# The state's part of y in one float32r pass, two chunks at once, with D's product inside the addition

## The chip, the cores and the metric

The kernel runs on one core of one Trainium2 chip. The metric is the device time of one execution in microseconds (us), as the median of the runs. Five engines work side by side, each in its own order: TensorE (PE, with its weight loads listed as PEld), VectorE (DVE), ScalarE (ACT), GpSimd (POOL) and SyncE (SP), which here issues all DMA transfers. An engine takes its instructions in the order in which they were written and waits at an instruction until what that one needs is there.

## The reference

Input x is 8 sequences of 2048 tokens of 256 numbers. One layer is a Mamba-like mixer and a feed-forward part with weights and activations rounded to a 4-bit grid, each followed by a residual addition and a layer norm:

```python
xz = x @ W_in                                   # 256 -> 2 x 512
x_proj, z = jnp.split(xz, 2, axis=-1)
x_conv = silu(conv4(x_proj) + conv_b)           # 512 channels, four taps, causal
ssm = x_conv @ W_xproj                          # 512 -> 1 + 16 + 16
delta = softplus(ssm[..., 0])
Bm, Cm = ssm[..., 1:17], ssm[..., 17:]
h_mean = einsum('bld,bln->bdn', x_conv, delta[..., None] * Bm) / L
y = einsum('bdn,bln->bld', h_mean, Cm)          # the state's part of y
y = y + D * x_conv
x = layernorm(x + (y * silu(z)) @ W_out)
# gate, up and down: fp4_linear, 256 -> 704 -> 256, and the second layernorm
```

So h_mean, a matrix of 512 channels by 16 numbers for each sequence, is known only when all 2048 tokens of the sequence have gone through the convolution. Only then can the state's part of y be worked out for any of its tokens.

## The kernel before

**Tiles.** The tokens are taken in 32 blocks of 512, four to a sequence (a batch). Channels lie on the 128 partitions in four chunks (`NC` = 4). A block's steps up to the sums over tokens (`begin_block`) are done four blocks ahead (`LAG`) of its state and finish: `mix_block` adds the state's part, and `finish_pair` does two halves of 256 tokens (gating, output projection, layer norm, rounding to the 4-bit grid, gate, up, down, layer norm, store). Between the two, the convolved block waits in `xc`, and C in `ct`.

**Order.** Nothing is scheduled by rule: each step has a place in a table (`BLOCK` and `PAIR` for the steady part, `FIRST`, `BEGIN`, `END`, `FINAL`, `LAST`, `PREPARE` for the two ends). A place is a number on a scale on which one block is 64. All steps are sorted by it and written out in that order, which is the order of every engine's queue. The places are thus an order, not times.

**The steps around the change.**
- `x_projection` (line 860) leaves B, C and delta's input of a block in one PSUM bank of 128x128: 32 partitions for each of four groups of tokens, with C in the first 16. A token's group is given by bits 5 and 6 of its number, in pieces of 32 tokens.
- `keep_ssm` (line 870) copies that to `ct` with ScalarE.
- `sums` (line 954) adds delta*B times x_conv over a block's tokens in TensorE; dB, the product of delta and B, comes from VectorE (line 883).
- With the last block of a sequence, `mean` (line 964) and `low_mean` (line 968) split h_mean into a float32r part and a float32r remainder. `spread_mean` (line 981) adds the four groups and copies the sum to all four groups of 32 partitions, in two float32r matmuls of 512 columns. `keep_mean` (line 991) copies that to `hT`.
- `state` (line 1042) has, for each chunk and each group of tokens, one float32 matmul with 16 rows and 128 columns; the four groups use four row groups of TensorE and four PSUM banks. A float32 matmul shows as two records, a float32r matmul as one.
- `skip` (line 994) multiplies x_conv by D in place with ScalarE, a chunk at a time.
- `mix` (line 1053) adds a bank of the state's part to `xc` with VectorE, a group of tokens at a time.
- After that come `gated` (line 1107, GpSimd) and the output projection (line 1114).

Other lines that the text names: the taps of the convolution (834, VectorE), projections of x and z (814, 1091), gate and up (1140), down (1192), its tails in float32r (1202), `low_tails` (1180), a residual addition (774), the normalization ahead of the rounding (485), the 4-bit scales' way through DRAM to all partitions (`q_rows` at 548, then `xqT` or `hqT` at 555), the transposes of the rounded numbers (`q_gT`, 562) and GpSimd's product of the two (565).

Of the kernel before, what the change touches and what calls it, by code (L numbers as in the profile page):

```python
# [8 lines left out]
F32 = mybir.dt.float32  # L9
# [8 lines left out]
P = 128  # L18
# [15 lines left out]
    "load": -52.34,  # L34
    "halo": (-54.39, 2.45, -18.45, 6.59),
    "project": (-14.43, 9.80, 37.20, 16.89),
    "fetch": (-7.60, 24.33, 44.39, 30.03),
    "first": (11.35, 35.33, 60.30, 30.38),
    "tap": ((18.88, 21.74, 37.66), (52.75, 58.32, 69.30), (67.71, 70.25, 77.19), (50.68, 57.97, 63.17)),
    "silu": (53.41, 75.33, 79.81, 69.00),  # L40
    "skip": (190.70, 157.15, 101.00, 177.52),
    "x_projection": 84.55,
    "keep_ssm": 92.56,
    "by_token": 100.69,
    "negate": 97.98,
    "exp": 100.76,
    "ratio": 102.43,
    "series": (105.64, 108.25),
    "delta": 110.56,
    "delta_b": 114.03,  # L50
    "turn": (62.70, 87.06, 88.65, 77.94),
    "turned": (76.69, 88.95, 91.00, 81.01),
    "sums": 128.76,
    "mean": 129.42,
    "spread_mean": 131.69,
    "keep_mean": 133.74,
    "state": 70.98,
    "mix": (73.82, 73.78, 77.92, 79.02),
    "weigh": (96.23, 96.41, 93.68, 93.73),
    "split": (57.98, 77.03, 86.29, 75.12),  # L60
    "low_mean": 129.60,
}
PAIR = {
    "load_t": (16.12, 22.16),
    "load_x": (59.79, 95.09),
    "zed": ((39.34, 27.02), (56.07, 45.07)),
    "silu_z": ((47.44, 31.13), (65.03, 56.88)),
    "gated": ((85.61, 79.64), (91.67, 86.97)),
    "out": (90.71, 124.00),
    "residual1": (94.73, 128.83),  # L70
    "n1_rstd": (102.55, 136.22),
    "n1_apply": ((103.52, 106.41), (137.06, 137.46)),
    "q1_scales": (107.95, 145.44),
    "q1_normalize": (108.65, 146.84),
    "q1_magnify": (110.07, 147.67),
    "q1_add": (114.27, 150.04),
    "q1_subtract": (116.81, 151.46),
    "q1_turn_scales": (108.81, 147.79),
    "q1_spread_scales": (117.33, 152.86),
    "q1_turn": (118.33, 156.58),  # L80
    "q1_scale": (129.34, 158.98),
    "gate": ((142.14, 140.98, 133.76), (167.27, 176.12, 174.04)),
    "silu_g": ((147.06, 144.40, 151.72), (171.89, 183.70, 186.46)),
    "up": ((144.69, 150.12, 147.67), (176.40, 172.28, 186.36)),
    "product": ((150.32, 154.57, 154.57), (187.42, 185.28, 189.04)),
    "q2_scales": (154.89, 189.41),
    "q2_normalize": (159.20, 196.57),
    "q2_magnify": (165.48, 200.74),
    "q2_add": (168.70, 206.24),
    "q2_subtract": (169.55, 207.52),  # L90
    "q2_turn_scales": (155.72, 193.80),
    "q2_spread_scales": (168.31, 201.20),
    "q2_turn": (174.65, 214.51),
    "q2_scale": (186.08, 215.81),
    "down": ((194.72, 203.27), (219.29, 220.91)),
    "residual2": (210.68, 227.83),
    "n2_rstd": (215.57, 239.09),
    "n2_apply": ((218.44, 218.00), (239.70, 241.77)),
    "store": (221.27, 244.14),
    "q1_gather_scales": (111.97, 152.22),  # L100
    "q2_gather_scales": (162.03, 196.03),
    "tails": ((203.00, 205.74), (226.14, 222.82)),
    "n1_means": (95.59, 131.31),
    "n1_squares": ((101.45, 99.66), (135.48, 132.20)),
    "n2_means": (211.12, 229.92),
    "n2_squares": ((213.85, 212.29), (235.64, 236.97)),
    "high_tails": (192.49, 220.15),
    "low_tails": (194.36, 220.71),
}
FIRST = {  # L110
    "load": -68.17,
    "halo": (8.02, -7.73, -7.47, 25.64),
    "project": (17.61, -14.66, 43.74, 34.99),
    "fetch": (19.36, 4.81, 51.19, 41.72),
    "first": (25.39, 17.49, 51.37),
    "tap": ((35.57, 38.38, 40.53), (34.74, 35.93, 60.13), (59.04, 70.58, 74.19)),
    "silu": (66.52, 68.87, 80.32, 71.88),
    "skip": (121.16, 219.05, 107.21, 100.33),
    "x_projection": 91.94,
    "keep_ssm": 98.65,  # L120
    "by_token": 98.83,
    "negate": 98.77,
    "exp": 100.23,
    "ratio": 102.34,
    "series": (102.95, 104.55),
    "delta": 105.72,
    "delta_b": 112.06,
    "turn": (85.02, 88.88, 84.23, 87.79),
    "turned": (107.58, 93.45, 91.94, 98.83),
    "sums": 121.00,  # L130
    "mean": 121.27,
    "spread_mean": 125.37,
    "keep_mean": 126.33,
    "state": 66.04,
    "mix": (71.99, 70.80, 70.83, 73.53),
    "weigh": (95.37, 97.80, 93.25, 96.77),
    "convolve": (49.83,),
    "low_mean": 124.04,
}
BEGIN = {  # L140
    "load_t": (-77.09, -0.67),
    "load_x": (-76.08, -1.35),
    "zed": ((60.35, -73.21), (31.76, 70.11)),
    "silu_z": ((72.40, 11.73), (47.63, 78.40)),
    "gated": ((80.54, 80.69), (84.07, 88.27)),
    "out": (81.29, 92.27),
    "residual1": (86.38, 98.03),
    "n1_rstd": (94.57, 110.77),
    "n1_apply": ((97.02, 95.31), (116.96, 119.50)),
    "q1_scales": (98.07, 122.11),  # L150
    "q1_normalize": (100.88, 130.91),
    "q1_magnify": (105.57, 137.37),
    "q1_add": (108.48, 137.49),
    "q1_subtract": (109.59, 138.28),
    "q1_turn_scales": (99.62, 127.03),
    "q1_spread_scales": (123.41, 136.86),
    "q1_turn": (125.14, 143.90),
    "q1_scale": (130.91, 151.54),
    "gate": ((133.56, 135.76, 146.80), (165.06, 172.15, 159.36)),
    "silu_g": ((148.69, 138.88, 150.75), (166.63, 175.38, 168.87)),  # L160
    "up": ((146.37, 143.27, 150.92), (169.68, 167.71, 162.37)),
    "product": ((153.21, 144.84, 155.15), (176.04, 175.47, 174.33)),
    "q2_scales": (155.98, 176.26),
    "q2_normalize": (156.45, 183.04),
    "q2_magnify": (162.10, 190.53),
    "q2_add": (165.07, 205.06),
    "q2_subtract": (170.07, 208.78),
    "q2_turn_scales": (157.57, 180.44),
    "q2_spread_scales": (169.87, 205.54),
    "q2_turn": (171.21, 208.80),  # L170
    "q2_scale": (181.69, 214.91),
    "down": ((186.77, 192.27), (221.73, 218.85)),
    "residual2": (198.55, 224.24),
    "n2_rstd": (210.52, 248.03),
    "n2_apply": ((216.78, 217.63), (250.34, 248.54)),
    "store": (222.03, 255.31),
    "q1_gather_scales": (111.97, 130.96),
    "q2_gather_scales": (161.52, 194.72),
    "tails": ((196.33, 196.65), (222.82, 224.20)),
    "n1_means": (89.02, 102.14),  # L180
    "n1_squares": ((90.01, 89.31), (107.12, 107.30)),
    "n2_means": (200.27, 237.43),
    "n2_squares": ((202.63, 208.26), (239.28, 238.86)),
    "high_tails": (184.10, 219.50),
    "low_tails": (192.85, 220.11),
}
END = {
    "load_t": (39.80, 13.28),
    "load_x": (84.06, 104.01),
    "zed": ((41.20, 45.87), (75.26, 70.21)),  # L190
    "silu_z": ((44.31, 77.44), (86.40, 71.48)),
    "gated": ((71.40, 84.31), (99.83, 102.23)),
    "out": (90.92, 104.08),
    "residual1": (94.66, 118.60),
    "n1_rstd": (100.60, 122.75),
    "n1_apply": ((103.01, 106.23), (134.03, 135.73)),
    "q1_scales": (106.61, 139.28),
    "q1_normalize": (115.25, 147.28),
    "q1_magnify": (125.29, 148.05),
    "q1_add": (128.25, 151.13),  # L200
    "q1_subtract": (136.11, 152.97),
    "q1_turn_scales": (111.18, 139.87),
    "q1_spread_scales": (140.92, 155.72),
    "q1_turn": (142.30, 156.65),
    "q1_scale": (144.67, 159.64),
    "gate": ((148.01, 187.75, 209.32), (169.60, 163.63, 165.58)),
    "silu_g": ((150.66, 199.52, 212.85), (173.05, 197.11, 186.69)),
    "up": ((159.27, 174.74, 209.62), (171.44, 192.91, 187.62)),
    "product": ((176.55, 218.42, 251.49), (177.96, 200.34, 189.33)),
    "q2_scales": (254.96, 204.69),  # L210
    "q2_normalize": (255.50, 211.67),
    "q2_magnify": (294.36, 235.57),
    "q2_add": (295.01, 276.85),
    "q2_subtract": (318.60, 304.87),
    "q2_turn_scales": (256.75, 207.35),
    "q2_spread_scales": (316.27, 314.21),
    "q2_turn": (383.51, 327.55),
    "q2_scale": (415.11, 334.42),
    "down": ((507.19, 550.28), (361.85, 374.70)),
# [76 lines left out]
def mamba_fp4_ffn_kernel(  # L296
# [735 lines left out]
    def mix_block(n):  # L1032
# [24 lines left out]
        for t in range(TT):  # L1057
            at((n + LAG) * PERIOD, table, "mix", (t,), mix, t)
# [407 lines left out]
```

## Time and profile before

| | |
|---|---|
| median of 3 runs | 1766.36 us (1766.3 to 1766.78) |
| the profiled execution | 1770.15 us, its span 1768.4 us |
| granted TensorE clock | 0.997 |
| TensorE busy | 1736.7 us in 9646 records |
| VectorE busy | 1587.0 us |
| ScalarE busy | 1166.6 us |
| GpSimd busy | 778.3 us |
| state, line 1042 | 1024 records, 37.5 us busy |
| mix, line 1053 | 128 instructions, 83.7 us, 681 ns each |
| skip, line 994 | 128 instructions, 91.7 us, 717 ns each |

The span runs from the first to the last instruction of the profiled execution; the execution's own time has 1.75 us around it. Busy time of TensorE is the union of its records, whose ends are modelled: starts are the better measure there. Idle time of an engine is put down to whatever released it last.

### The profile page before, as it was taken

How to read it: one execution, taken by the hardware profiler on the slowest of the kernel's cores; microseconds unless marked ns; L12 is line 12 of the kernel's file. 1: busy time of each engine (PE TensorE's matmuls, PEld its weight loads, DVE VectorE, ACT ScalarE, POOL GpSimd, SP SyncE). 2: the span in 40 equal slices, each digit the busy share in tenths (PEclk: the TensorE clock that was granted, in tenths of full speed). 3: DMA queues.
4: the chain of work that ended last, by engine and by line, in shares of the span. 5: the costliest groups of instructions: out<-in, count | busy, mean ns of one | idle time of the engine just before them, and what ended most of it. 6: DMA issues, size and time to landing. Idle time of an engine off the chain costs nothing.

```text
span 1768.4 us, 28454 instructions
## 1 busy us (share of the span) xinstructions
PE 1736.7 (98%) x9646; PEld 1397.9 (79%) x9646; DVE 1587.0 (90%) x3081; ACT 1166.6 (66%) x2371; POOL 778.3 (44%) x840
## 2 busy tenths in 40 slices
PE   7999999999999999999999999999999999999997
PEld 3568787888877788788788888788888788888886
DVE  5998999998989999999999999999999999977786
ACT  5786767666767666767666767666777666654444
POOL 2333554444444444544444544444444444545443
PEclk9999999999999999999999999999999999999999
DMA  3244565555656555656655656554665545555443
GB/s 109 72 95 100 120 125 118 120 106 115 132 112 125 120 103 115 126 122 126 114 103 120 124 124 126 114 106 117 126 123 124 114 101 111 123 106 114 99 89 74
DMA packets 367473, 199.46 MB, mean 113 GB/s; under 512 B 290272, under 2 KB 342368, under 8 KB 367328
## 3 DMA queue, kind: packets, MB, share of 16 engines
q1 hardware_dynamic: 367328, 197.65, 53.5%
q8 instruction: 76, 1.25, 0.3%
q14 instruction: 69, 0.57, 0.1%
HBM read 116.34 MB, written 20.91 MB: 78 GB/s over the span
## 4 chain that ended last, share of the span: by engine, by line
PE 85%; DVE 8%; DMA 2%; ACT 2%; POOL 1%; issue 1%; SPq 0%; ACTq 0%; POOLq 0%; DVEq 0%
PE ps L1140 31%; PE ps L1192 14%; PE ps L1114 11%; PE ps L1091 11%; PE ps L814 10%; DVE xc L834 2%; PE ps L1042 2%; PE ps L1202 2%; PE hsum L954 2%; PE ps L860 1%; DMA hwT<-hw 1%; DVE xd L940 1%; DVE q_x L485 1%; DMA q_gT<-q_w 1%; DVE q_x L497 0%
## 5 line engine op out<-in xcount | busy, mean ns | idle before, releaser
L834 DVE SCALAR_TENSOR_TENSOR xc<-xp,cw_sb,xc 128x512 f32<-128x512 f32 x372 | 357.6, 983 | 9.7 <-ACT xc L828 9.1
L1140 PE MATMUL ps<-wuT,xqT 128*128 128x256 f32 (+1 forms) x1512 | 331.0, 363 | 1.5 <-ACT sg L1158 1.5
L1140 PE MATMUL ps<-wgT,xqT 128*128 128x256 f32 (+1 forms) x1512 | 326.5, 363 | 3.8 <-POOL xqT L565 3.8
L1140 PEld LDWEIGHTS ps<-wuT,xqT 128*128 128x128 f32 x1512 | 274.3, 190 | 46.2 <-issue 11.4
L1140 PEld LDWEIGHTS ps<-wgT,xqT 128*128 128x128 f32 x1512 | 273.5, 191 | 41.8 <-issue 12.2
L1192 PE MATMUL ps<-wdT,hqT 128*128 128x256 f32 x1260 | 290.7, 381 | 0.5 <-POOL hqT L565 0.5
L1192 PEld LDWEIGHTS ps<-wdT,hqT 128*128 128x128 f32 x1260 | 234.6, 190 | 51.8 <-issue 16.8
L1107 POOL TENSOR_TENSOR xc<-xc,sz 128x512 f32<-128x512 f32 x128 | 216.5, 1711 | 115.2 <-DVE xc L1053 115.2
L814 PE MATMUL ps<-xT,w_in_sb 128*128 128x512 f32 x512 | 245.9, 606 | 7.6 <-DMA xT<-in_x_t_dram 7.6
L1091 PE MATMUL ps<-xTz,w_in_sb 128*128 128x256 f32 x1024 | 242.1, 379 | 0.0
L1114 PE MATMUL ps<-w_out_sb,xc 128*128 128x256 f32 x1008 | 228.2, 379 | 2.2 <-DVE h L1165 1.9
L1091 PEld LDWEIGHTS ps<-xTz,w_in_sb 128*128 128x128 f32 x1024 | 194.0, 190 | 39.4 <-issue 14.4
L758 ACT ACTIVATE x<-x,ln_nb,ln_rs 128x256 f32<-128x256 f32 x256 | 142.4, 593 | 117.2 <-POOL ln_nb L755 97.6
L1114 PEld LDWEIGHTS ps<-w_out_sb,xc 128*128 128x128 f32 x1008 | 190.3, 190 | 28.7 <-issue 2.7
L565 POOL TENSOR_TENSOR hqT<-q_gT,hqT 128x1408 f32<-128x1408 bf16 x63 | 187.6, 2978 | 47.0 <-DMA q_gT<-q_w 40.0
L497 DVE SCALAR_TENSOR_TENSOR q_x<-q_w,q_x 128x512 f32<-128x512 bf16 (+3 forms) x131 | 156.1, 1192 | 39.8 <-ACT q_w L493 39.7
L493 ACT ACTIVATE q_w<-q_x 128x512 bf16<-128x512 f32 (+3 forms) x131 | 130.2, 994 | 86.8 <-DVE q_x L485 86.6
L907 ACT COPY xct<-hwT 128x1024 uint16<-128x1024 uint16 x112 | 130.0, 1161 | 83.1 <-DMA hwT<-hw 83.0
L814 PEld LDWEIGHTS ps<-xT,w_in_sb 128*128 128x128 f32 x512 | 94.0, 193 | 85.5 <-issue 77.7
L501 DVE SCALAR_TENSOR_TENSOR q_w<-q_w,q_x 128x512 bf16<-128x512 bf16 (+3 forms) x131 | 157.7, 1204 | 1.4
L565 POOL TENSOR_TENSOR xqT<-q_gT,xqT 128x512 f32<-128x512 bf16 x63 | 77.9, 1236 | 183.6 <-DMA q_gT<-q_w 173.5
L1165 DVE TENSOR_TENSOR h<-sg,ps 128x512 f32<-128x512 f32 (+1 forms) x189 | 116.7, 636 | 44.3 <-PE ps L1140 35.7
(137 smaller groups left out, 2548.9 us busy)
## 6 DMA issues: line engine op xcount, KB each, us to landing
hqT<-q_rows SPq DMA_DIRECT2D x63, 704.0 KB
xT<-in_x_t_dram SPq DMA_DIRECT2D x32, 512.0 KB
xTz<-in_x_t_dram SPq DMA_DIRECT2D x64, 256.0 KB
xt<-in_L_attn_x_dram SPq DMA_DIRECT2D x64, 256.0 KB
xqT<-q_rows SPq DMA_DIRECT2D x63, 256.0 KB
out_dram<-x SPq DMA_DIRECT2D x63, 256.0 KB
q_rows<-q_scT SPq DMA_DIRECT2D x252, 4.0 KB
q_rows<-q_scT SPq DMA_DIRECT2D x252, 12.0 KB
```

What stands on the lines that cost most here:

```text
L493: nc.scalar.activation(state["g"], state["x"], AF.Abs, scale=GRID)
L497: nc.vector.scalar_tensor_tensor(xn, w, 1.5 * GRID, xn, ALU.max, ALU.subtract)
L501: nc.vector.scalar_tensor_tensor(w, w, 1.5 * GRID, xn, ALU.max, ALU.subtract)
L565: nc.gpsimd.tensor_tensor(qT(), state["gT"], qT(), ALU.mult)
L758: nc.scalar.activation(r()[:, t, :], r()[:, t, :], AF.Identity, bias=v["nb"][:, t : t + 1], scale=v["rstd"][:, t : t + 1],)
L814: nc.tensor.matmul(mm, w_in_sb[:, k, c * P : (c + 1) * P], s["xT"][:, k, :], start=(k == 0), stop=(k == KM - 1),)
L834: nc.vector.scalar_tensor_tensor(acc, xp[:, k + 1 : k + 1 + T], cw_sb[:, c, k + 1 : k + 2], acc, ALU.mult, ALU.add)
L1091: nc.tensor.matmul(q["mm", j][:, a, :], w_in_sb[:, k, DI + c * P : DI + (c + 1) * P], q["xT"][:, k, :], start=(k == 0), stop=(k == KM - 1),)
L1107: nc.gpsimd.tensor_tensor(xc, xc, q["sz"][:, c, :], ALU.mult)
L1114: nc.tensor.matmul(mm[:, t, :], s["xc"][:, c, o : o + P], w_out_sb[:, c, :], start=(c == 0), stop=(c == NC - 1),)
L1140: nc.tensor.matmul(q[name, j][:, t, :n], q["xqT"][:, t * KM + k, :], wT[:, k, f0 : f0 + n], start=(k == 0), stop=(k == KM - 1),)
L1192: nc.tensor.matmul(q["d"][t], q["hqT"][:, t * (NF + 1) + j, :], wdT[t][:, t + j, :], start=(j == 0), stop=False,)
```

## The change

1. **C is split and spread.** `keep_ssm` still fills `ct`, for the transpose in `by_token` alone. `high` (ScalarE) copies the block's projection as float32r, `low` (VectorE) takes the remainder. `put_parts` writes C's two parts to DRAM in four transfers; some three blocks later `get_parts` reads them back in two transfers into `cs`: 64 partitions (16 numbers, by two parts, by two copies), 512 tokens in each row, and the same again in the other half of the partitions.
2. **h_mean is laid out to match.** `spread` now copies each of the 16 numbers to four rows in both halves of the partitions. `keep_mean` keeps the float32r part of all rows, and a new step `part_mean` (VectorE) turns the odd rows into the remainder. So the 64 rows of a half hold the four products of parts.
3. **state** is four float32r matmuls of 64 rows and 512 columns, one for each chunk, alternating between the lower and the upper half of the partitions. Each has a PSUM bank of its own.
4. **mix** goes by chunks, and multiplies `xc` by D as it adds: one `scalar_tensor_tensor`. `skip` is gone.
5. `xd` has two buffers instead of one, `ct` two instead of six, and **every table of places is new**.

```diff
 def keep_ssm():
-    s["ct"] = keep.tile([P, P], F32, tag="ct", name="ct")
-    nc.scalar.copy(s["ct"], s.pop("mm"))
+    s["ct"] = p2.tile([P, P], F32, tag="ct", name="ct")
+    nc.scalar.copy(s["ct"], s["mm"])
+
+def high():
+    s["hl"] = p2.tile([P, 2, P], F32, tag="hl", name="hl")
+    nc.scalar.copy(s["hl"][:, 0, :].bitcast(F32R), s["mm"])
+
+def low():
+    hl = s["hl"]
+    nc.vector.tensor_tensor(
+        hl[:, 1, :].bitcast(F32R), s.pop("mm"), hl[:, 0, :], ALU.subtract
+    )
+
+def put_parts():
+    s["parts"] = dram.tile([DS, 2, TT, P], F32, tag="parts", name="parts", bufs=LAG + 2)
+    hl = s.pop("hl")
+    for g in range(TT):
+        nc.sync.dma_start(s["parts"][:, :, g, :], hl[g * G : g * G + DS])
+
+def get_parts():
+    s["cs"] = p2.tile([P, TT, P], F32, tag="cs", name="cs")
+    rows = s.pop("parts").rearrange("n h g t -> (n h) (g t)")
+    for half in range(2):
+        nc.sync.dma_start(
+            s["cs"][half * 2 * G : (half + 1) * 2 * G].rearrange("p g t -> p (g t)"),
+            rows.unsqueeze(1).to_broadcast([G, 2, T]),
+        )
...
 def keep_mean():
-    hT_of[b] = p2.tile([P, DI], F32, tag="hT", name="hT", bufs=1)
-    nc.scalar.copy(hT_of[b], hs_of.pop("mm"))
-
-def skip(c):
-    nc.scalar.activation(
-        s["xc"][:, c, :], s["xc"][:, c, :], AF.Copy, scale=dk_sb[:, c : c + 1]
-    )
+    hs_of["high"] = p2.tile([P, 2, DI], F32, tag="hs", name="h_high", bufs=1)[:, 0, :]
+    nc.scalar.copy(hs_of["high"].bitcast(F32R), hs_of["mm"])
+
+def part_mean():
+    hT_of[b] = p2.tile([P, DI], F32, tag="hT", name="hT", bufs=1)
+    nc.vector.scalar_tensor_tensor(
+        hT_of[b].bitcast(F32R), hs_of.pop("high"), low_rows, hs_of.pop("mm"),
+        ALU.mult, ALU.add,
+    )
...
 def state():
-    s["y"] = [bank().rearrange("p (c n) -> p c n", n=P) for _ in range(TT)]
-    for c in range(NC):
-        for t in range(TT):
-            g = slice(t * G, t * G + DS)
+    s["y"] = [bank() for _ in range(NC)]
+    cs = s.pop("cs").rearrange("p g (t r) -> p t g r", r=G)
+    for j in range(NC // 2):
+        for half in range(2):
+            c = half * (NC // 2) + j
+            g = slice(half * 2 * G, (half + 1) * 2 * G)
             nc.tensor.matmul(
-                s["y"][t][:, c, :],
-                hT_of[b][g, c * P : (c + 1) * P],
-                s["ct"][g, :],
+                s["y"][c],
+                hT_of[b][g, c * P : (c + 1) * P].bitcast(F32R),
+                cs[g].bitcast(F32R),
                 start=True, stop=True,
             )

-def mix(g):
-    xc = s["xc"].rearrange("p c (t g r) -> p g c t r", g=TT, r=G)[:, g]
-    y = s["y"][g].rearrange("p c (t r) -> p c t r", r=G)
-    nc.vector.tensor_tensor(xc, xc, y, ALU.add)
+def mix(c):
+    xc = s["xc"][:, c, :]
+    nc.vector.scalar_tensor_tensor(
+        xc, xc, dk_sb[:, c : c + 1], s["y"][c], ALU.mult, ALU.add
+    )
```

The new `spread` and `low_rows` (minus one in odd rows, zero in even ones) are made once at the start by three small VectorE instructions more.

## The prediction, made before the changed kernel ran

> **What bounds the kernel now.** I read the page first (busy shares, the 40 slices, the chain that ended last), then the waits of TensorE, then stretches of the span, then TensorE's order of work around the lines that change.
>
> ```profile
> span 1768.4 us, 28454 instructions
> PE 1736.7 (98%) x9646; PEld 1397.9 (79%) x9646; DVE 1587.0 (90%) x3081; ACT 1166.6 (66%) x2371; POOL 778.3 (44%) x840
> PE 85%; DVE 8%; DMA 2%; ACT 2%; POOL 1%; issue 1%; SPq 0%; ACTq 0%; POOLq 0%; DVEq 0%
> ```
> TensorE is busy 98% of the span, and the chain runs through it for 85%. What an instruction on another engine costs matters only if TensorE then waits.
>
> The busy time of each engine in a stretch of the middle, in the order TensorE, weight load, VectorE, ScalarE, GpSimd, with clock, DMA share and GB/s:
> ```profile
> 200.00:460.00 260.00, 260.00 (x1460) 210.26 (x1459) 240.47 (x466) 180.01 (x363) 119.62 (x124) 1.00 0.59 118
> ```
> There TensorE never stops, at full clock, and a block takes 53.0 us. VectorE works 92.5% of that, 49.0 us a block: 4 us of room. TensorE's idle 31.7 us lie at the two ends of the span; the waits name 7.6 for the first load and 4.0 for dB at the start, and 1 to 2 each at the end.
>
> The price of the state's part is in TensorE's timeline (start, us, line, what, count):
> ```profile
> 545.68 1.46 PE L1140 MATMUL ps<-wgT,xqT 128*128 128x192 f32 x8
> 547.08 1.17 PE L1042 MATMUL ps<-ct,hT 16*128 16x128 f32 x32
> 548.18 1.98 PE L814 MATMUL ps<-xT,w_in_sb 128*128 128x512 f32 x4
> ...
> 515.96 4.48 PE L1192 MATMUL ps<-wdT,hqT 128*128 128x256 f32 x20
> 520.09 0.83 PE L1202 MATMUL ps<-wd_parts,parts 128*128 128x256 f32 x4
> 520.76 1.88 PE L814 MATMUL ps<-xT,w_in_sb 128*128 128x512 f32 x4
> ```
> A float32 matmul is two records. From start to start the 32 records of line 1042 take 1.10 us. The eight of 192 columns ahead take 1.40, though elsewhere in the steady part eight of them take 1.30, and a run of ten of line 1192 after such a state takes 2.26 (1675.03 to 1677.29) where 2.15 is usual. So the state costs TensorE 1.10 + 0.10 + 0.11 = 1.31 us a block. Its work proper, eight rounds of four row groups at once, each round 256 column steps, is eight times 0.115 = 0.92 us by the price of such steps below; the other 0.4 us go to entering and leaving.
>
> **The change, part by part.**
>
> *State in float32r, two halves of rows at once.* A float32r matmul is one record. Line 1202 is the nearest row: 20 records of line 1192 at 0.2155 last until 520.27, so the four float32r passes of 256 columns fill 520.27 to 520.76, 0.12 each; 512 columns are 0.23 to 0.24 (line 981, the only 512-column float32r row, gives 0.46 for two by the same reckoning). The four new passes use rows 0 to 63 and 64 to 127 alternately. Two at once: two rounds, 0.46 + 0.40 = 0.86 us. Bounds: 0.46 without any entering and leaving; 4 x 0.23 + 0.40 = 1.32 if the halves don't run together. I take 0.86, since line 1042 itself shows row groups together (32 records of over 0.1 us of steps in 1.10 us). Saved: 1.31 - 0.86 = 0.45 us a block, times 32 blocks: **-14.4 us**, at most -27.
>
> A rule of the Trainium skill speaks against a part of it. The row: while line 1202 runs, its weight loads (0.19 us each) start 0.12 to 0.19 us apart with passes of the same rows in flight, so a load is hidden.
> "TensorE: Matmul & The Clock Gate", Part 3, says that a weight load overlaps matmuls in flight only where the row group differs. By it the third pass would wait for its 0.19 us load, and 6 us of the 14.4 would be lost.
> I go by the row.
>
> *D joins the addition.* ScalarE loses 128 activations of 0.717 (line 994), 91.7 us; it gains 32 copies of 128x128 (row of line 870: 0.258), 8.3 us. It has a third of its time free, so nothing on the path. VectorE's four additions a block become multiply-adds of the same size: line 1053 takes 0.681, line 968 (the same form, 512 wide, one operand in PSUM) 0.690: +1.2 us in all. The nearest row that could be dearer is line 834, 0.983 with both operands in SBUF, which would be +39; but lines 968 and 774 read PSUM as the new one does and never exceed 0.70 and 0.43.
>
> *Split of C.* VectorE gains 32 subtractions of 128x128: between 0.28 (line 1180, 64x128) and 0.69 (line 968, 512 wide); I take 0.29, 9 us in all. Ahead of the transposes and additions in its queue that is 0.3 us in 4 of room: no cost. Without that room it would be 9 us.
>
> *The way through DRAM.* Six more transfers a block on SP: four writes, as line 548's four (1.7 to 2.6 us of issue), and two reads of 128 KB each. The writes stand behind the store and ahead of the q_rows and xt issues, and wait for the subtraction; the reads stand between the q_rows issue and the issue of xqT, which waits for q_rows anyway:
> ```profile
> 637.23 1.73 SPq L548 DMA_DIRECT2D q_rows<-q_scT  x4
> 639.85 0.40 SPq L1217 DMA_DIRECT2D out_dram<-x  x1
> 640.43 0.62 SPq L555 DMA_DIRECT2D xqT<-q_rows  x1
> 643.09 1.23 SPq L562 DMA_TRANSPOSE q_gT<-q_w  x1
> ```
> xqT is issued 2.6 us before the transpose that GpSimd's product also needs, and that product ends 3 to 6.7 us before TensorE uses it. One microsecond later costs nothing; without cover it would be 1 us a block, 32 us. The q_rows behind the writes feed hqT, whose issue (625.90) came 8 us before its transpose's (634.47). The reads come some three blocks after their writes.
>
> *The start of a batch.* The state of its first block waits for hT, and the way there gets one step longer, a VectorE multiply-add of 0.69 (row of line 968), behind the copy. Before:
> ```profile
> 1547.65 0.81 PE L981 MATMUL ps<-hs,spread 128*128 128x512 f32 x2
> 1548.30 1.46 PE L1140 MATMUL ps<-wgT,xqT 128*128 128x192 f32 x8
> 1549.70 1.17 PE L1042 MATMUL ps<-ct,hT 16*128 16x128 f32 x32
> ...
> 1548.50 0.59 ACT L991 COPY hT<-ps 128x512 f32<-128x512 f32 x1 [0.47 <-PE ps L981]
> 1548.61 1.63 DVE L485 TENSOR_TENSOR q_x<-h,q_rs 128x1408 f32<-128x1408 f32 x1
> ```
> hT was there at 1549.09. In the new order VectorE runs low_mean, then that 1.63 us normalization, then the new step. Low_mean ended at 1547.76, so the new step runs from 1549.4 to 1550.1. TensorE, with two more passes of line 1202 ahead of the state (0.24 us), is ready at 1549.8: a wait of 0.3 us, eight times: **+2.4 us**. Bounds 0 and 1.6 (another such operation) each: 0 to 13.
>
> *New places.* The steady order keeps its distances. Adding TensorE's rows: from the end of the output projection to the first gate matmul 30.5 and 33.4 us by halves (30.5 and 32.2 before), from the last up matmul to the first down 33.0 and 33.8 (31.8 and 29.1 before), from the state to the output projection 15.4 (15.5). At the start, block 0's x projection stands 10.8 us ahead of its sums instead of 8.6, which should give back some 2 of the 3.7 us that TensorE waits there. At the end the last pairs have 1 to 2 us less between up and down; I count +2. Together 0, with 4 either way.
>
> **Sum.** -14.4 + 2.4 = -12.0. The profiled execution took 1770.15 (span 1768.4 and 1.75 around it), so 1758 for one like it; it lies 3.8 above the median of the runs, 1766.36. That median less 12.0 is 1754.4: **1754.5 us**.
>
> **The rivals.**
> 1. *The halves don't run together, or the 128-byte pieces in which a pass reads C halve its pace.* Line 860 reads such pieces without loss, but in float32, at half the rate of columns. The state then costs 1.32, nothing is won, and the start of a batch adds 2.4: 1769. For it: no row here shows 64-row groups. Against: line 1042 shows four row groups together.
> 2. *The batch starts eat the gain.* VectorE arrives a whole long operation late at each: 8 x 1.6 = 13 us, so 1766. Against: only the queue's next operation stands there, of known length.
> 3. *VectorE becomes the bound* (slower). It goes from 49.0 to about 49.5 us a block. Its twelve taps a block average 0.98 us, between 0.65 and 3.4, whatever their equal shape; the long ones lie beside other engines' work. If new neighbours raise that mean, the blocks follow VectorE once it needs 52.6, a mean of 1.24; beyond 1.32 the kernel is slower than before. At 1.35 it needs 53.9, 0.9 over the old period in 28 steady blocks: 1791. For it: 4 us of room and every place new. Against: TensorE's waits on VectorE in the steady part are zero now, and ScalarE and GpSimd get no more work.
>
> **How the numbers follow.** A measurement of this kernel tells differences over about 0.2% (3.5 us) from none. Forecast 0.68, its own range 1746 to 1763 (the run at 0.6 to 1.0, ends 4 either way); rival 1 0.12, rival 2 0.05, rival 3 0.15. Faster: the forecast and 0.03 of rivals 1 and 2 in part, 0.71. Same: 0.12. Slower: rival 3 and the worst of rival 1, 0.17. The range reaches to rivals 1 and 2, 1745 to 1772, and leaves rival 3 out.
>
> **What would show it.** Right: the state as four records that start in two close pairs, with about 0.66 us from its start to the next line's in place of 1.10, TensorE's share still 98%, steady period 52.5 us, small waits on hT at batch starts. Wrong: four records 0.23 apart (rival 1), waits on hT of over 1 us (2), a tap mean over 1.2 us and TensorE waiting for VectorE in the middle (3), or TensorE waiting for the read-back C or for xqT, which would put the six transfers on the path.

## The result, and the profile after

The changed kernel takes 1788.0 us (median of 4, 1785.8 to 1789.2) beside 1766.6 us for the kernel before: a ratio of 1.0119, with a 95% interval of 1.0102 to 1.0137. It is slower by 21 us, where 12 us less were forecast. The profiled execution took 1786.9 us, its span is 1785.1 us, the granted clock 0.994.

The head of the page and the shares of the chain that ended last, after:

```profile
span 1785.1 us, 26935 instructions
PE 1732.8 (97%) x8750; PEld 1383.5 (78%) x8750; DVE 1658.4 (93%) x3123; ACT 1099.8 (62%) x2275; POOL 794.5 (45%) x840
DVE 49%; PE 22%; ACT 12%; issue 9%; POOL 4%; DMA 3%; SPq 0%; DVEq 0%; ACTq 0%; POOLq 0%
```
TensorE's part of the chain fell from 85% to 22%, VectorE's rose from 8% to 49%. VectorE is busy for 71 us more than before, though the new instructions are few and small.

The same stretch of the middle as in the prediction, and TensorE's timeline around a state (line 1098 now):

```profile
200.00:460.00 260.00, 253.71 (x1289) 201.79 (x1288) 250.85 (x455) 165.25 (x335) 117.36 (x118) 1.00 0.62 124
```
```profile
544.97 0.53 PE L1259 MATMUL ps<-wd_parts,parts 128*128 128x256 f32 x2
545.44 0.73 PE L1098 MATMUL ps<-cs,hT 64*128 64x512 f32 x4
546.10 1.99 PE L1197 MATMUL ps<-wgT,xqT 128*128 128x256 f32 x8
```
The state is what the forecast said: four records that start in two close pairs, 0.34 us apart, and 0.66 us from its start to the next line's (545.44 to 546.10) in place of 1.10. But TensorE, which never stopped in this stretch before, now stops for 6.3 us of it, and VectorE works 96.5% of it.

Where VectorE's 71 us went is in its groups with shapes kept apart (busy us, mean ns). The lines of before, then of after; each second line is the subtraction of the first quantization, line 501 before and 520 after:

```profile
L834 DVE SCALAR_TENSOR_TENSOR xc<-xp,cw_sb,xc 128x512 f32<-128x512 f32 x372 | 357.6, 983 | 9.7 <-ACT xc L828 9.1
L501 DVE SCALAR_TENSOR_TENSOR q_w<-q_w,q_x 128x512 bf16<-128x512 bf16 x63 | 49.2, 781 | 0.2
L1053 DVE TENSOR_TENSOR xc<-xc,ps 128x512 f32<-128x512 f32 x128 | 83.7, 681 | 7.8 <-PE ps L1042 7.4
```
```profile
L853 DVE SCALAR_TENSOR_TENSOR xc<-xp,cw_sb,xc 128x512 f32<-128x512 f32 x372 | 334.7, 920 | 8.5 <-ACT xc L847 8.2
L520 DVE SCALAR_TENSOR_TENSOR q_w<-q_w,q_x 128x512 bf16<-128x512 bf16 x63 | 134.5, 2134 | 1.2
L1108 DVE SCALAR_TENSOR_TENSOR xc<-xc,dk_sb,ps 128x512 f32<-128x512 f32 x128 | 91.9, 741 | 14.4 <-PE ps L1098 14.3
L897 DVE TENSOR_TENSOR hl<-ps,hl 128x128 fp32r<-128x128 f32 x32 | 8.3, 258 | 0.2
```
The new work (line 897, 8.3 us; 8.2 us more in the additions; 5.9 us for the part of the mean) is some 22 us. The taps got shorter. One instruction that the change does not touch, the subtraction of line 520, went from 0.78 to 2.13 us and took 85 us more: 33 of its 63 now last over 2.5 us, where 2 did before.

Its neighbours show why. GpSimd's and VectorE's timelines of after, at the same time (start, us):

```profile
614.50 2.87 POOL L584 TENSOR_TENSOR hqT<-q_gT,hqT 128x1408 f32<-128x1408 bf16 x1
```
```profile
614.52 3.40 DVE L520 SCALAR_TENSOR_TENSOR q_w<-q_w,q_x 128x512 bf16<-128x512 bf16 x1
617.85 1.14 DVE L1222 TENSOR_TENSOR h<-sg,ps 128x512 f32<-128x512 f32 x2
```
The subtraction lasts until 0.55 us after GpSimd's product into `hqT` is over. Alone it takes 0.68 us. So it stood still for about 2.7 us, and the profile counts that as busy time. The next pair of products waits behind it. In the kernel before, the subtraction (line 501) was out of the way when that product (line 565) began:

```profile
615.53 0.70 DVE L501 SCALAR_TENSOR_TENSOR q_w<-q_w,q_x 128x512 bf16<-128x512 bf16 x1
617.78 1.15 DVE L1165 TENSOR_TENSOR h<-sg,ps 128x512 f32<-128x512 f32 x2 [1.55 <-PE ps L1140]
```
```profile
617.03 2.88 POOL L565 TENSOR_TENSOR hqT<-q_gT,hqT 128x1408 f32<-128x1408 bf16 x1
```
There GpSimd's product lay in a gap of VectorE and beside two products with one operand in PSUM, which took no longer than elsewhere. Other `hqT` products held a tap, then as now at the cost of some 2.7 us (23 taps of over 2.5 us before, 15 after): those are the longest taps of the prediction.

### The profile page after: what moved, and what is told of

It reads as the page before. It is cut to its first block, busy times and chain, and to the rows that moved or that the text cites. A ratio compares the mean times of both kernels' runs of the same rounds, so it can differ in the third digit from the quotient of the medians.

```text
span 1785.1 us, 26935 instructions
## 1 busy us (share of the span) xinstructions
PE 1732.8 (97%) x8750; PEld 1383.5 (78%) x8750; DVE 1658.4 (93%) x3123; ACT 1099.8 (62%) x2275; POOL 794.5 (45%) x840
## 4 chain that ended last, share of the span: by engine, by line
DVE 49%; PE 22%; ACT 12%; issue 9%; POOL 4%; DMA 3%; SPq 0%; DVEq 0%; ACTq 0%; POOLq 0%
DVE xc L853 11%; PE ps L1197 8%; DVE q_x L516 5%; DVE q_am L483 5%; DVE q_w L520 4%; DVE h L1222 4%; DVE xd L984 4%; DVE q_x L504 3%; PE ps L1249 3%; ACT xct L951 3%; PE ps L833 3%; PE ps L1148 3%; PE ps L1171 2%; DVE q_sc L490 2%; DVE x L793 2%
## 5 line engine op out<-in xcount | busy, mean ns | idle before, releaser
L1197 PE MATMUL ps<-wgT,xqT 128*128 128x256 f32 (+1 forms) x1512 | 337.9, 367 | 5.3 <-issue 3.5
L853 DVE SCALAR_TENSOR_TENSOR xc<-xp,cw_sb,xc 128x512 f32<-128x512 f32 x372 | 334.7, 920 | 8.5 <-ACT xc L847 8.2
L1197 PE MATMUL ps<-wuT,xqT 128*128 128x256 f32 (+1 forms) x1512 | 324.3, 361 | 0.0
L1164 POOL TENSOR_TENSOR xc<-xc,sz 128x512 f32<-128x512 f32 x128 | 223.2, 1755 | 119.6 <-DVE xc L1108 119.5
L584 POOL TENSOR_TENSOR hqT<-q_gT,hqT 128x1408 f32<-128x1408 bf16 x63 | 192.9, 3061 | 119.6 <-DMA q_gT<-q_w 82.2
L520 DVE SCALAR_TENSOR_TENSOR q_w<-q_w,q_x 128x512 bf16<-128x512 bf16 (+3 forms) x131 | 242.2, 1849 | 1.4
L770 POOL TENSOR_SCALAR ln_ve<-ln_var 128x2 f32<-128x2 f32 (+1 forms) x130 | 50.9, 392 | 288.4 <-ACT ln_sq L759 282.8
L1159 ACT ACTIVATE sz<-ps 128x512 f32<-128x512 f32 x128 | 76.0, 593 | 143.9 <-PE ps L1148 143.4
```

The source lines that it names most:

```text
L520: nc.vector.scalar_tensor_tensor(w, w, 1.5 * GRID, xn, ALU.max, ALU.subtract)
L584: nc.gpsimd.tensor_tensor(qT(), state["gT"], qT(), ALU.mult)
L853: nc.vector.scalar_tensor_tensor(acc, xp[:, k + 1 : k + 1 + T], cw_sb[:, c, k + 1 : k + 2], acc, ALU.mult, ALU.add)
L1164: nc.gpsimd.tensor_tensor(xc, xc, q["sz"][:, c, :], ALU.mult)
L1197: nc.tensor.matmul(q[name, j][:, t, :n], q["xqT"][:, t * KM + k, :], wT[:, k, f0 : f0 + n], start=(k == 0), stop=(k == KM - 1),)
```

## The experiments

Theory P: the new places put a VectorE instruction beside GpSimd's product that holds it; the change's own arithmetic is as cheap as forecast. Rival W: the change gives VectorE more work than it has room for. All kernels of this section were timed against the kernel before (medians 1766.4 to 1767.4 us). "Start", "middle" and "end" split the span at the first matmul of the fifth and of the last block's state, as the trace has them. "Batch start" and "other" are the mean intervals from one state to the next over 22 blocks, beginning at the fifth: the 5 intervals that lead to the first block of a new sequence, and the other 17. VectorE's busy time and the subtraction's mean are in us.

| kernel | us | ratio (95%) | VectorE busy | subtraction, mean | start | middle | end | batch start | other |
|---|---|---|---|---|---|---|---|---|---|
| before | 1766.4 | | 1587 | 0.78 | 281.2 | 1392.7 | 94.5 | 53.43 | 53.10 |
| after | 1788.0 | 1.0119 (1.0102 to 1.0137) | 1658 | 2.13 | 275.1 | 1415.7 | 94.3 | 57.09 | 53.18 |
| e1, places alone | 1790.9 | 1.0133 (1.0118 to 1.0148) | 1643 | 1.90 | 277.8 | 1412.6 | 95.6 | 55.60 | 53.40 |
| e2, arithmetic alone | 1781.2 | 1.0086 (1.0069 to 1.0103) | 1575 | 0.70 | 286.2 | 1399.0 | 94.7 | 55.31 | 52.93 |
| e3, products first | 1753.9 | 0.9927 (0.9912 to 0.9942) | 1617 | 1.41 | 271.0 | 1388.2 | 95.6 | 54.22 | 52.60 |
| e4, no hqT product | 1740.8 | 0.9852 (0.9836 to 0.9869) | 1543 | 1.20 | 267.1 | 1378.9 | 92.8 | 53.05 | 52.58 |
| e5, hqT on VectorE | 1772.1 | 1.0026 (1.0015 to 1.0037) | 1607 | 0.70 | 271.8 | 1394.3 | 104.1 | 55.19 | 52.66 |
| e6, mean earlier | 1748.7 | 0.9898 (0.9881 to 0.9914) | 1617 | 1.47 | 268.6 | 1381.2 | 94.4 | 53.40 | 52.61 |
| e7, e5 and e6 | 1761.4 | 0.9969 (0.9959 to 0.9980) | 1605 | 0.70 | 272.7 | 1385.2 | 104.2 | 53.74 | 52.60 |
| e8, mean earlier alone | 1778.2 | 1.0065 (1.0050 to 1.0080) | 1663 | 2.19 | 270.4 | 1411.4 | 94.6 | 54.93 | 53.62 |
| e9, gating first | 1754.7 | 0.9931 (0.9914 to 0.9948) | 1619 | 1.45 | 273.9 | 1386.7 | 93.2 | 54.25 | 52.58 |
| e10, mixed orders | 1748.0 | 0.9890 (0.9874 to 0.9906) | 1607 | 1.25 | 271.5 | 1381.9 | 92.8 | 53.40 | 52.58 |
| e11, part of the mean first | 1769.9 | 1.0021 (1.0010 to 1.0033) | 1571 | 0.70 | 284.8 | 1388.5 | 93.3 | 53.53 | 52.85 |

**e1: the new places, without the new arithmetic.** The kernel of before, with every table of the changed kernel (`skip` keeps its own places). In its first block the gating of the first half comes ahead of the last of the four additions, since the new tables go by chunks.

> The kernel of before, with the changed kernel's places for every step that both have; no new arithmetic. Theory P (the new places: the VectorE subtraction of q1 stands beside GpSimd's product into hqT and lasts until that is over): the subtraction's mean goes from 0.78 us to 1.5 to 2.2 us, VectorE's busy time from 1587 us to 1630 to 1660 us; TensorE still needs its old 53.2 us a block, so that most of this lies beside it, and the time is 1768 to 1782 us. Theory W (the change's own VectorE work - the remainder of C, D inside the mix, the part of the mean - is too much for VectorE): the subtraction stays at 0.78 us, VectorE at 1587 us within 10, the time at 1766 us within 4.

Measured 1790.9 us. The subtraction's mean is 1.90 us and VectorE is busy for 1643 us, as P said and W did not. The time is above P's range: I had counted the holds as lying beside TensorE's 53.1 us. TensorE waits at the batch starts instead, 55.6 us there beside 53.4 us. There is no added link in this kernel, yet TensorE stops for 8.1 us in all, in `spread_mean`, until VectorE has the remainder of the mean. So the places alone, on old arithmetic, cost 24 us.

**e2: the new arithmetic, with the old places.**

```diff
 BLOCK (all other places as before)
+    "high": 93.24, "low": 95.07, "put_parts": 97.46, "get_parts": 311.72, "part_mean": 134.20,
+    "mix": (73.78, 77.92, 73.82, 79.02),
-    "skip": ...
```

> The changed kernel's arithmetic, with the places of before for every step that both have, and the new steps (the two parts of C, their store and read-back, the part of the mean) put in where the changed kernel has them relative to their neighbours. P: the subtraction's mean is 0.7 to 0.9 us, VectorE is busy for 1590 to 1615 us, TensorE's state passes are 0.44 us shorter a block, and the time is 1750 to 1762 us, 5 to 16 us under before. W: VectorE is busy for 1640 us or more and the time is 1780 us or more, as in the changed kernel.

Measured 1781.2 us, where W put it (1780 us or more) and above P's range. But W's reason is not there: VectorE is busy for 1575 us, less than before, and the subtraction takes 0.70 us. The blocks within a sequence take 52.93 us, 0.17 less than before. The loss is elsewhere: 5 us in the first blocks, and at the batch starts, where TensorE waits for the new link of the mean's chain. TensorE's timeline, then VectorE's:

```profile
928.95 0.80 PE L1098 MATMUL ps<-cs,hT 64*128 64x512 f32 x4 [1.74 <-DVE hT L1039]
```
```profile
925.96 1.62 DVE L504 TENSOR_TENSOR q_x<-h,q_rs 128x1408 f32<-128x1408 f32 x1
927.50 0.74 DVE L853 SCALAR_TENSOR_TENSOR xc<-xp,cw_sb,xc 128x512 f32<-128x512 f32 x1
928.16 0.74 DVE L1039 SCALAR_TENSOR_TENSOR hT<-h_high,low_rows,ps 128x512 fp32r<-128x512 f32 x1
```
This is the second rival of the prediction, under the old order: the part of the mean stands behind a normalization and a tap, and the state's matmuls wait 1.7 us. Three of these waits are followed by 3.4 us in which the granted clock is 0.50, which takes another 1.7 us each.

**e11: the same, with the normalization behind the part of the mean.** `"q2_normalize"` of the second half goes from 196.57 to 198.21.

> The changed kernel's arithmetic with the places of before (1781.2 us), and on VectorE the normalization of the second half's second quantization (1.62 us) moved behind the new part of the mean, which it stood ahead of. There the state's matmuls waited 1.7 to 2.2 us for hT at seven batch starts, and the block before a start took 54.8 to 57.2 us. If the new link of the chain, queued behind that normalization, is what costs there: 53.0 to 53.6 us at the starts and 1767 to 1774 us in all. If the rest (the first blocks, single blocks of 54.3 us) weighs more, or the wait only moves to another matmul: 1777 to 1782 us.

Measured 1769.9 us, 11 us less than e2. The batch starts fall from 55.31 to 53.53 us. One place of one instruction, which runs once a block, decided whether the added link was on the path. It is still 3.5 us over the kernel before: the start is 3.6 us longer and a block takes 52.85 us, not 52.58. What keeps it there was not taken apart.

**e3: VectorE's order around the subtraction.** In the second half of a block the subtraction goes behind the two products; in the first half behind the products and ahead of two taps.

```diff
-    "q1_subtract": (117.96, 153.46),
+    "q1_subtract": (122.06, 158.28),
-    "q1_turn": (126.15, 155.03),
+    "q1_turn": (126.15, 158.29),
-    "tap": (..., (49.63, 54.48, 64.97), ..., (51.31, 54.87, 64.83)),
+    "tap": (..., (49.63, 58.10, 64.97), ..., (51.31, 58.20, 64.83)),
```

> The changed kernel, with only VectorE's order around the two q1 subtractions of a steady block altered: the two products of gate and up, which read one operand from PSUM, go ahead of the subtraction, so that they and not the subtraction run beside GpSimd's product into hqT (in one of the two places two taps also move behind the subtraction). No work is taken away. P: the subtraction still waits for the rest of hqT's product, but about 1.1 us of it is used twice a block; the subtraction's mean falls from 2.13 to 1.2 to 1.7 us, VectorE is busy for 1590 to 1625 us, and the time is 1758 to 1774 us. W: the work is the same, so the time stays at 1788 us within 4 and VectorE at 1658 us within 10.

Measured 1753.9 us, below P's range, 34 us under the changed kernel, with the same instructions. VectorE's busy time fell by 42 us, and W falls.

**e9: GpSimd's order alone.** The changed kernel with one place moved: in one half of a block the gating (1.3 us) goes ahead of `hqT`'s product. The orders of the other engines are untouched.

```diff
-    "q2_scale": (185.89, 217.49),
+    "q2_scale": (185.89, 222.20),
```

> The changed kernel (1788 us) with one place altered, on GpSimd's queue alone: in one of the two halves of a block the gating product (1.3 us) goes ahead of hqT's product (2.9 us). VectorE's, ScalarE's and TensorE's orders are those of the changed kernel. H (a VectorE instruction with both operands in SBUF is held for as long as GpSimd's product runs): in that half the q1 subtraction stands beside the gating instead and is held for 1 us and not 2.7 us; hqT's product then runs beside the two products with a PSUM operand and the maximum, which are not held; the subtraction's mean falls from 2.13 us to 1.2 to 1.7 us and the time to 1766 to 1780 us. O (the products-first kernel was faster only because VectorE reads the gate and up results out of PSUM earlier): VectorE's order is unchanged here, so the subtraction and the time stay, 1788 us within 3.

Measured 1754.7 us: 33 us under the changed kernel, more than H had expected, and O is out. That the gating itself comes earlier isn't the gain: TensorE never waited for it in the changed kernel. GpSimd's and VectorE's timelines, to be held against 614.50 above:

```profile
605.62 1.27 POOL L1164 TENSOR_TENSOR xc<-xc,sz 128x512 f32<-128x512 f32 x1
606.86 3.32 POOL L584 TENSOR_TENSOR hqT<-q_gT,hqT 128x1408 f32<-128x1408 bf16 x1
```
```profile
605.64 1.80 DVE L520 SCALAR_TENSOR_TENSOR q_w<-q_w,q_x 128x512 bf16<-128x512 bf16 x1
607.36 1.14 DVE L1222 TENSOR_TENSOR h<-sg,ps 128x512 f32<-128x512 f32 x2
608.54 1.62 DVE L483 TENSOR_REDUCE q_am<-h 128x88 f32<-128x1408 f32 x1
```
The subtraction is held by the gating for 1.1 us instead of by the product for 2.7, and the product runs beside instructions that it does not hold. The chain turned back to TensorE:

```profile
PE 82%; DVE 13%; issue 2%; ACT 1%; POOL 1%; DMA 0%; SPq 0%; DVEq 0%; ACTq 0%; POOLq 0%
```

**e4: GpSimd's product into hqT left out.**

```diff
 def scale():
-    nc.gpsimd.tensor_tensor(qT(), state["gT"], qT(), ALU.mult)
+    if n != NT * FF:
+        nc.gpsimd.tensor_tensor(qT(), state["gT"], qT(), ALU.mult)
```

> The changed kernel, with GpSimd's product into hqT left out (64 instructions of about 3 us; the second quantization's values are not put into hqT, which keeps the scales alone); all VectorE instructions stay, in their order. P: nothing is left that holds the subtraction, its mean is 0.70 to 0.80 us, VectorE is busy for 1540 to 1580 us, the period of a block is 52.5 us and the time 1748 to 1760 us. W: VectorE has the same instructions and stays the bound, the time is 1780 us or more; a fall to 1770 us or less speaks against it.

Measured 1740.8 us, below P's range. VectorE, with every instruction still there, is busy for 1543 us, 116 less. The subtraction's mean is 1.20 us, not the 0.7 to 0.8 expected: the gating holds it now. The kernel also has the results of that product sooner, but TensorE's waits for GpSimd's products were 1.9 us in all in the changed kernel, little beside the 47 us that are gone. The blocks take 52.58 us, 0.52 less than before, and the batch starts 53.05. So the forecast's two terms on TensorE (0.45 a block less, 0.3 more at a batch's start) hold once VectorE is in time.

**e5: hqT's product on VectorE, from e3.** `nc.vector` in place of `nc.gpsimd` for that product, with places behind the subtraction and the products.

> The kernel with the products first (1753.9 us), and the product into hqT issued on VectorE behind the two products and the subtraction, not on GpSimd. H (it is the holding that costs: a VectorE instruction with two operands in SBUF stands still while GpSimd's long product runs): VectorE gets 63 instructions of about 1.62 us more (as the 128x1408 rows of q_x), 102 us, but nothing is held by hqT any more, so that its busy time is 1630 to 1650 us, over the 1616 us of the products-first kernel, and the time all the same falls to 1743 to 1752 us. S (it is VectorE's sum of busy time that sets the time): with more busy time than in the products-first kernel the time rises to 1755 us or more.

Measured 1772.1 us, 18 more than e3, in S's range and not in H's. But S's reason is not there: VectorE's busy time is lower than in e3 (1607 beside 1617 us), `hqT`'s product holds no subtraction (0.70 us), and the blocks within a sequence take 52.66 us as they do in e3. The loss is 8.5 us at the end of the kernel and 1 us at each batch start. That the places there, made for GpSimd's product, do not suit VectorE's is my guess; it was not tried. My expectation had missed that e3's blocks were already at TensorE's pace, so that there was nothing left to win in them.

**e6 and e8: the mean's chain a few places earlier,** from e3 and from the changed kernel:

```diff
-    "mean": 130.53, "low_mean": 132.49, "part_mean": 133.43,
+    "mean": 128.68, "low_mean": 129.86, "part_mean": 133.22,
```

> The kernel with the products first (1753.9 us), and at the start of a batch the chain of the mean a few places earlier: ScalarE's copy ahead of the silu and the tails, VectorE's remainder ahead of the second addition of the residual, the part of the mean ahead of the normalization of the second quantization. In that kernel the block before a batch's first takes 53.7 to 55.3 us where the others take 52.5 us, with 0.6 to 1.8 us between the two matmuls that spread the mean. If the order around the chain causes it: 53.0 to 53.4 us at those seven places, 5 to 9 us less in all, 1745 to 1750 us. If VectorE is simply late there: the wait moves to the state's matmuls and the time stays at 1754 us within 2.

> The changed kernel (1788 us), with nothing but the chain of the mean moved as in the run before; the subtractions of q1 stay beside hqT's product. If the chain's length itself is the cause (my rival with the batch starts): the gaps of about 2.3 us at eight starts go, 1768 to 1776 us. If VectorE's lateness is the cause and the batch starts are only where TensorE meets it: the waits move to the tails and the state's matmuls, 1780 to 1788 us.

e6 takes 1748.7 us, 5 less than e3; the batch starts fall to 53.40 us. e8 takes 1778.2 us, between the two expectations. Its batch starts fall from 57.09 to 54.93 us, but the other blocks rise from 53.18 to 53.62 us: over half of the wait only moved. In TensorE's timeline of the changed kernel, at such a start, both links of the chain come late, one from ScalarE and one from VectorE:

```profile
921.31 0.49 PE L1025 MATMUL ps<-hs,spread 128*128 128x512 f32 x1 [0.71 <-ACT hs L1008]
923.09 0.79 PE L1025 MATMUL ps<-hs,spread 128*128 128x512 f32 x1 [1.29 <-DVE hs L1012]
```

**e7: e5 and e6 together.**

> The products first, hqT's product on VectorE and the chain of the mean earlier, together. If holding and the order around the chain are the two causes, both gains add up: 1737 to 1746 us, TensorE's period 52.5 us in the steady blocks and 53.0 to 53.3 us at a batch's start. If VectorE's sum of work is the bound: 1755 us or more.

Measured 1761.4 us. That is in the second expectation's range, but VectorE's sum of work isn't the bound: it is busy for 1605 us, less than in e6, and the blocks within a sequence take 52.60 us. The gain at the batch starts is there (53.74 us), and so are the 8.5 us more at the end.

**e10: e6 with e9's order in place of the products first,** in that half of the block.

> The kernel with the mean's chain earlier (1748.7 us), with the half of the gating altered as in the run before in place of the products first. H: both ways free VectorE from one hold in that half, so VectorE's busy time stays within 30 us of 1617 us, TensorE stays the bound at 52.5 us a block, and the time is 1746 to 1755 us. O: 1760 us or more.

Measured 1748.0 us, 1.1% under the kernel before, the fastest of the kernels that do the whole work; e6 lies within its spread. TensorE carries 88% of the chain again:

```profile
PE 88%; DVE 7%; POOL 1%; ACT 1%; issue 1%; DMA 1%; SPq 0%; ACTq 0%; POOLq 0%; DVEq 0%
```

## Why the prediction was wrong

**The step that failed is "New places": "The steady order keeps its distances ... Together 0, with 4 either way".** It was worked out from TensorE's rows alone. The places alone, on the old arithmetic, cost 24 us (e1). The traces of before and after, 17 us apart, split the difference into 6 us won at the start, 23 us lost in the middle and nothing at the end. I had not gone through which VectorE instruction the new order puts beside which GpSimd product, and that decides: e9 moves one GpSimd instruction past another and takes 33 us back.

**The row that told it was in the text.** The prediction saw taps of one shape last between 0.65 and 3.4 us, "beside other engines' work", and turned that into a risk for the taps. A time like that belongs to a pair of instructions, not to the taps. The longest lasted as long as GpSimd's product beside them, so any VectorE instruction of that kind could be the next. After, it was the subtraction; in e9 it is dB, whose mean is 1.14 us beside 0.22 before.

**"4 us of room" on VectorE was too generous.** VectorE's own new work was nearly right: 22 us in all, 0.7 us a block where I had 0.5; D inside the additions took 8.2 us, where I had 1.2. The holds made it 51.7 us a block (95.7% of the mean interval of 54.07 us), under the 52.6 at which I let it become the bound. It led the chain all the same (49%). But the share of busy time doesn't decide this: in e6 VectorE is busy for the same 95.7% (50.5 of 52.79 us), and TensorE leads with 79%. What counts is which instruction comes late behind a hold. In the changed kernel these are the tails' parts and the parts of the mean:

```profile
PE ps L1259 <- DVE parts L1237: 11.6, 10, 2.4
PE ps L1025 <- DVE hs L1012: 6.4, 5, 1.3
PE ps L1025 <- ACT hs L1008: 5.8, 6, 1.5
```
These are TensorE's waits there: for what, us in all, times, the longest.

**Rival 3 was right in engine and sign, wrong in the instruction, and its price came out by luck.** It gave a period of 53.9 us for every steady block, and 1791 us; the mean period is 54.07 and the time 1788. But that mean is made of 53.18 us within a sequence, 0.08 more than before, and 57.09 at the batch starts, where the rival put nothing special. (By its own sum VectorE reaches the old period of 53.0 us at a tap mean of 1.27 us, not 1.32.) Its sign to look for, a tap mean over 1.2 us, did not come (0.92). Its second sign did: TensorE waits for VectorE in the middle. Its chance of 0.15 rested on "ScalarE and GpSimd get no more work". GpSimd got none; its product only moved beside another neighbour.

**Batch starts: +0.3 us each was right only with VectorE in time.** With e4 the start costs 0.47 us over the other blocks, beside 0.33 before. In the changed kernel it costs 3.9. There TensorE stops in `spread_mean` (line 1025), for both parts of the mean, and never at the state for `hT`: the added link is not what costs. With fewer holds (e3) the start takes 54.22 us instead of 57.09, and with the mean's chain earlier as well (e6) 53.40. The added link costs under the old order: rival 2 priced it at 1.6 us, and e2 shows a wait of 1.7 us.

A stop there costs more than the wait. After four of these batch starts the granted clock is 0.50 for 3.4 us, here after the first of the four (start, length, then TensorE, weight load, VectorE, ScalarE, GpSimd, clock, DMA share, GB/s):

```profile
489.40:492.80 3.40, 3.40 (x11) 3.18 (x11) 2.01 (x2) 2.75 (x7) 0.90 (x2) 0.50 1.27 177
```
Eight matmuls of 192 columns that follow the stop take 2.3 us there, where 1.3 is usual. Half the clock for 3.4 us is 1.7 us lost, so the four make up 6.8 of the 23 us of the middle. In the middle of the kernel before, of e3, e6 and e10, and of e1, whose stops there are 1.3 us each, the clock never fell. That the longer stops bring the lower clock is what this suggests; no run was made for it.

**The state's term was right.** In e4, e9 and e10 the blocks take 52.58 us instead of 53.10: 0.52 less, where I had 0.45. The rule of the Trainium skill in "TensorE: Matmul & The Clock Gate", Part 3, by which 6 of the forecast's 14.4 us would be lost, is not what these runs show; the row of line 1202, whose weight loads start 0.12 to 0.22 us apart in the trace, was the better guide. Rival 1 is out by the two close pairs. No wait of TensorE in the changed kernel names C's way through DRAM or ScalarE's new copies.

**The forecast's number came back for partly other reasons.** e3 and e9 take 1754, as forecast. But only 4.5 and 6.0 us of it come from the middle; 10 and 7 us come from the start, where I had counted 2. e10 has the forecast's middle (10.8 us less) and a start that is 9.7 us shorter on top. Part of this is the clock: in the kernel before it was 0.50 for 3.4 us twice in the first 130 us, which takes 3.4 us; at the start of e3 and e10 that happened never, in e9 once. Which of the new places bring the rest was not taken apart.

## What to carry to other kernels

Where instructions of one shape have very different times, list what GpSimd does beside the long ones before pricing any change of order; then go through the new order pair by pair, for every VectorE instruction with both operands in SBUF. Put GpSimd's long products beside VectorE instructions that read PSUM, or beside its reductions, or into its gaps. And read "busy" on VectorE with suspicion: time in which it is held counts as busy, so a full engine may need another neighbour rather than less work. Then look for the next instruction behind the hold that TensorE waits for, and at the granted clock just after such a stop.

## What the runs showed of the hardware

I had not expected an instruction of 0.68 us to last 3.40 us because another engine works. The runs show the kind of it. Held until GpSimd's end were instructions with two operands in SBUF: the subtraction and a tap (3.37 us), which ended 0.55 us after it, and even dB, 128x64 in size (2.90 us instead of 0.22), which ended 0.08 us after it. A multiplication by a constant with one operand was held too (line 490, beside the product into `xqT`, until 0.07 us after its end):

```profile
620.59 1.16 POOL L584 TENSOR_TENSOR xqT<-q_gT,xqT 128x512 f32<-128x512 bf16 x1 [1.53 <-PE ps L833]
```
```profile
620.67 1.15 DVE L490 TENSOR_SCALAR q_sc<-q_am 128x96 f32<-128x96 f32 x1
```
Where nothing held it, the same instruction took 0.21 us. Not held were the products with an operand in PSUM, the additions of line 1108 (0.74 us) and the maximum of line 483 (1.62 us in e9 beside `hqT`, as elsewhere). It also goes the other way: in e9 the product, starting 0.58 us before the end of the subtraction, took 3.32 us instead of 2.87.

The Trainium skill has this in "SBUF — State Buffer", section "Who interferes with whom": a VectorE instruction with two SBUF inputs contends with a GpSimd instruction that reads SBUF, and the one that comes second is blocked until the first is through; reductions never are. The trace of before already agreed, with taps of up to 3.4 us, and I did not bring the two together.
